# Output columns of a head on the quarter of its sums: the inverses of a softmax without a change of partition

## The chip, the cores and the metric

One core of a Trainium2 chip runs the whole kernel. The metric is the device time of one execution in microseconds (us); lower is better. Times are medians of several executions, and all runs compared here are in the fast state (granted TensorE clock 0.993 to 0.997 of full speed, averaged over a run).

## The reference, cut to what matters

Sixty-four batches of a 256 x 512 float32 matrix go through two layers. The first is multi-head attention over a graph with a residual and a layer norm, the second a graph convolution with the same. Only the attention is touched:

```python
q = (x @ Wq + bq).reshape(b, n, H, HD)                   # H = 8 heads, HD = 64
k = (x @ Wk + bk).reshape(b, n, H, HD)
v = (x @ Wv + bv).reshape(b, n, H, HD)
scores = jnp.einsum('bqhd,bkhd->bhqk', q, k) / jnp.sqrt(jnp.float32(HD))
scores = scores + (1.0 - adj)[None, None, :, :] * -1000000000.0
attn = jax.nn.softmax(scores, axis=-1)
out = jnp.einsum('bhqk,bkhd->bqhd', attn, v).reshape(b, n, d)
return out @ Wo + bo
# ... then x = layernorm(x + that), and a second layer of the same build
```

## The kernel before

It works on pairs of batches, 32 of them. A pair has four units, each one batch and one group of four heads. TensorE multiplies the values of a unit with the exponentials in four column groups of 32, side by side, each into its own quarter of the 128 partitions; it also sums the exponentials of each head into one quarter. In the kernel before, two neighbouring quarters belong to the two halves of one head, so that the sums of a head do not always stand where its outputs stand. Five small copies on ScalarE carry the inverse sums (1 over a sum of exponentials, by which softmax divides) to the quarters that need them:

```python
    def values(p, u):
        ...
        for a in range(2):
            for kc in range(NC):
                for s in range(2):
                    for r in range(2):
                        q, h = s * HD + r * 32, (2 * a + s) * HD + r * 32
                        nc.tensor.matmul(at[q:q + 32, 0, a, :], V[p, g][:, kc, b, h:h + 32], e[kc][:, s, a, :],
                                         start=kc == 0, stop=kc == NC - 1)
        for s in range(2):
            for a in range(2):
                q = s * HD + a * 32
                nc.tensor.matmul(at[q:q + 32, 1, 0, :], ones[:, 0:32], sm[:, s, a, :], start=True, stop=True)
        later(1, divided, p, u, at)

    def divided(p, u, at):
        ...
        nc.vector.transpose(z, at[:, 1, 0, :])                       # 256 elements per partition
        z1 = z.rearrange("p (j k) -> p j k", k=32)[:, :, 0]
        nc.vector.reciprocal(rz1, z1)
        nc.scalar.activation(rz, rz1[:, None, :].to_broadcast([P, 2, 8]), AF.Copy)
        for s in range(2):
            for a in range(2):
                here, there = (slice(s * HD + r * 32, s * HD + r * 32 + 32) for r in (a, 1 - a))
                nc.scalar.activation(rz[there, a], rz1[here], AF.Copy)
        nc.vector.transpose(rs, rz...)                               # 512 elements per partition
        nc.vector.tensor_tensor(O[p, g]..., at[:, 0]..., rs..., op=OP.mult)
        ...
```

ScalarE also reads the products of q out of PSUM, the memory into which TensorE writes; such a reading is called an eviction below. The kernel forms q from seven products of blocks and of sums of blocks. The third of them adds into the PSUM bank of the first, so it has to wait until the first was read:

```python
    SEVEN = [("a11", 0, 0, True), ("a12", 1, 1, True), ("s2", 4, 0, False), ...]   # name, block of w, bank, begins
    ...
        def first(to, pm, g):                                        # in q_or_k
            for a in range(2):
                nc.scalar.activation(to[:, a], pm[:, a], AF.Identity, bias=b[:, 2 * g + a:2 * g + a + 1])
```

The order of instructions on each engine is fixed when the kernel is built, by a scheduler that works with its own idea of when each operation is ready. At the start, VectorE forms four sums of blocks for each weight matrix, in the same queue as its additions to q, k and v.

Of the kernel before, what the change touches and what calls it, by code (L numbers as in the profile page):

```python
# [20 lines left out]
F32 = mybir.dt.float32  # L21
AF = mybir.ActivationFunctionType
OP = mybir.AluOpType
AX = mybir.AxisListType

P = 128
# [7 lines left out]
def tile_adj_resnorm(tc, x, adj, wq, bq, wk, bk, wv, bv, wo, bo, w1, b1, out):  # L34
    good = fast(tc, x, adj, wq, bq, wk, bk, wv, bv, wo, bo, w1, b1, out)
    with tc.If(good < P):
        general(tc, x, adj, wq, bq, wk, bk, wv, bv, wo, bo, w1, b1, out)


def fast(tc, x, adj, wq, bq, wk, bk, wv, bv, wo, bo, w1, b1, out):  # L40

    nc = tc.nc
    B, N, D = x.shape
    HD = D // H
    DC = D // P
    NC = N // P
    T2 = 2 * N
    NP = B // 2
    HF = D // 2
# [10 lines left out]
    cpool = pool("consts", 1)  # L60
    xpool = pool("xp", 4)
    rpool = pool("rp", 2)
    one = pool("one", 1)
    qk = pool("qk", 3)
    four = pool("four", 4)
    small = pool("small", 2)
# [3 lines left out]
    XC, R, XT, Q, K, V, E, SM, O, Y, ST = ({} for _ in range(11))  # L70
# [14 lines left out]
    ident = cpool.tile([P, P], F32, name="ident")  # L85
    make_identity(nc, ident)

    def weights(w, name):

        t = cpool.tile([P, 7, 2, HF], F32, name=name)  # L90
        b12 = one.tile([P, 2, HF], F32, name="b12")
        quarter = lambda k, n: w[k * HF:(k + 1) * HF, n * HF:(n + 1) * HF].rearrange("(c p) e -> p c e", p=P)
        nc.sync.dma_start(b12, quarter(0, 1))
        for i, (k, n) in enumerate(((0, 0), (1, 0), (1, 1))):
            nc.sync.dma_start(t[:, i], quarter(k, n))
        return t, b12

    def weight_sums(t, b12):
        b11, b21, b22, t1, t2, t3, t4 = (t[:, i] for i in range(7))
        nc.vector.tensor_tensor(t1, b12, b11, op=OP.subtract)  # L100
        nc.vector.tensor_tensor(t2, b22, t1, op=OP.subtract)
        nc.vector.tensor_tensor(t3, b22, b12, op=OP.subtract)
        nc.vector.tensor_tensor(t4, b21, t2, op=OP.subtract)

    def by_partition(b, name):
        t = cpool.tile([P, DC], F32, name=name)
        nc.scalar.dma_start(t, b.rearrange("(c p) -> p c", p=P))
        return t
# [3 lines left out]
        nc.scalar.dma_start(t, b.partition_broadcast(P))  # L112
        return t

    bq_s, bk_s, bv_s = by_partition(bq, "bq"), by_partition(bk, "bk"), by_partition(bv, "bv")
    W = {}
    for name, w in (("v", wv), ("q", wq), ("k", wk)):
        W[name], b12 = weights(w, "w" + name)
        weight_sums(W[name], b12)
# [3 lines left out]
    load_r(0)  # L123
    load_r(1)

    ones = cpool.tile([P, HD], F32, name="ones")
    nc.gpsimd.memset(ones, 1.0)
    power = cpool.tile([P, 4], F32, name="power")
    nc.gpsimd.memset(power, -0.5)
# [4 lines left out]
            nc.tensor.transpose(pt[:, mc, c * P:(c + 1) * P], adj_s[:, c, mc * P:(mc + 1) * P], ident)  # L134
    nc.vector.tensor_copy(adjT, pt)

    acc = cpool.tile([P, 16], F32, name="acc")
    square = one.tile([P, NC, N], F32, name="z")
    nc.vector.tensor_tensor(square, adj_s, adj_s, op=OP.mult)
    nc.vector.tensor_tensor(square, square, adj_s, op=OP.not_equal)  # L140
# [4 lines left out]
    def weights_of_outputs():  # L145
        W["1"], b12 = weights(w1, "w1")
        weight_sums(W["1"], b12)
        W["o"], b12 = weights(wo, "wo")
        weight_sums(W["o"], b12)

        wide = one.tile([P, DC, P], F32, name="z")
        nc.vector.tensor_copy(wide, bv_s[:, :, None].to_broadcast([P, DC, P]))
        pm = ps_mm.tile([P, 2, HF], F32, name="mm")
        for n, blocks in enumerate(((W["o"][:, 0], W["o"][:, 1]), (b12, W["o"][:, 2]))):
            for d in range(DC):
                nc.tensor.matmul(pm[:, n, :], wide[:, d, :], blocks[d // 2][:, d % 2, :], start=d == 0,
                                 stop=d == DC - 1)
        nc.vector.tensor_tensor(bo_s, bo_s, pm.rearrange("p n e -> p (n e)"), op=OP.add)
# [5 lines left out]
    def later(n, f, *args):  # L164
        due.append([n, f, args])

    def tick():
        for d in due:
            d[0] -= 1
        ready = [d for d in due if d[0] <= 0]  # L170
        due[:] = [d for d in due if d[0] > 0]
        for _, f, args in ready:
            f(*args)  # L173
# [7 lines left out]
    def row_sums(lo, hi, name):  # L181


        flat = lambda t: t.rearrange("p k b i -> p k (b i)")
        a11, a21, a12, a22 = flat(lo[:, 0]), flat(lo[:, 1]), flat(hi[:, 0]), flat(hi[:, 1])
        sums = one.tile([P, 3, 2, HF], F32, name=name)
        s1, s2, s4 = (sums[:, i] for i in range(3))
        for i, args in enumerate(((s1, a21, a22, OP.add), (s2, s1, a11, OP.subtract), (a21, a11, a21, OP.subtract),
                                  (s4, a12, s2, OP.subtract))):
            later(i + 1, nc.vector.tensor_tensor, *args)  # L190
        return dict(a11=a11, a12=a12, a22=a22, s1=s1, s2=s2, s3=a21, s4=s4)
# [71 lines left out]



    UNITS = [(g, b) for g in range(2) for b in range(2)]

    def scores(p, u):
        g, b = UNITS[u]
        for kc in range(NC):  # L270

            sc = ps_at.tile([P, 2, 2, N], F32, name="at")
            for a in range(2):
                for s in range(2):
                    r = slice(s * HD, (s + 1) * HD)
                    nc.tensor.matmul(sc[:, s, a, :], K[p, g][r, kc, a, b, :], Q[p, g][r, :, a, b, :],  # L276
                                     start=True, stop=True)
            e = E[p, u, kc] = one.tile([P, 2, 2, N], F32, name=f"e{kc}")
            nc.scalar.activation(e, sc, AF.Exp, scale=qscale)  # L279
            later(1 + kc, masked, p, u, kc)  # L280
# [11 lines left out]
    def values(p, u):  # L292
        g, b = UNITS[u]
        if (p, g) not in O:
            O[p, g] = four.tile([P, NC, 2, 2, P], F32, name="o")
        while (p, u) not in SM:
            tick()
        e = [E.pop((p, u, kc)) for kc in range(NC)]
        sm = SM.pop((p, u))
        at = ps_at.tile([P, 2, 2, N], F32, name="at")  # L300
        for a in range(2):
            for kc in range(NC):
                for s in range(2):
                    for r in range(2):
                        q, h = s * HD + r * 32, (2 * a + s) * HD + r * 32
                        nc.tensor.matmul(at[q:q + 32, 0, a, :], V[p, g][:, kc, b, h:h + 32], e[kc][:, s, a, :],  # L306
                                         start=kc == 0, stop=kc == NC - 1)
        for s in range(2):
            for a in range(2):
                q = s * HD + a * 32  # L310
                nc.tensor.matmul(at[q:q + 32, 1, 0, :], ones[:, 0:32], sm[:, s, a, :], start=True, stop=True)  # L311
        later(1, divided, p, u, at)

    def divided(p, u, at):


        g, b = UNITS[u]
        z = one.tile([P, N], F32, name="z")
        nc.vector.transpose(z, at[:, 1, 0, :])
        z1 = z.rearrange("p (j k) -> p j k", k=32)[:, :, 0]  # L320
        rz1 = small.tile([P, 8], F32, name="rz1")
        nc.vector.reciprocal(rz1, z1)  # L322
        rz = small.tile([P, 2, 8], F32, name="rz")
        nc.scalar.activation(rz, rz1[:, None, :].to_broadcast([P, 2, 8]), AF.Copy)  # L324
        for s in range(2):
            for a in range(2):
                here, there = (slice(s * HD + r * 32, s * HD + r * 32 + 32) for r in (a, 1 - a))
                nc.scalar.activation(rz[there, a], rz1[here], AF.Copy)  # L328
        rs = one.tile([P, T2], F32, name="rs")
        nc.vector.transpose(rs, rz.rearrange("p a j -> p (a j)")[:, :, None].to_broadcast([P, 16, 32]))  # L330
        nc.vector.tensor_tensor(O[p, g][:, :, :, b, :].rearrange("p c a i -> p a c i"), at[:, 0].rearrange("p a (c i) -> p a c i", c=NC),
                                rs.rearrange("p (a c i) -> p a c i", a=2, c=NC), op=OP.mult)
        seen = small.tile([P, 8], F32, name="seen")
        nc.gpsimd.tensor_tensor(seen, rz1, z1, op=OP.add)
        nc.gpsimd.tensor_tensor(acc[:, 0:8], acc[:, 0:8], seen, op=OP.add)
        if u == 3:
            O[p] = row_sums(O.pop((p, 0)), O.pop((p, 1)), "ys")

# [85 lines left out]
    for w in range(-1, NP + 1):  # L424
        steps = between(w)
        slots = [(f, w, u) for u in range(4) for f in (scores, values)] if 0 <= w < NP else []
        whole, done, n = sum(s[0] for s in steps), 0.0, len(slots)
        while steps or slots:
            if slots and done >= whole * (n - len(slots)) / n - 1e-6:
                f, p, u = slots.pop(0)  # L430
                f(p, u)
            elif steps:
                t, f, p, i = steps.pop(0)
# [3 lines left out]
            else:  # L437
                f, p, u = slots.pop(0)
# [4 lines left out]
    while due:  # L443
        tick()

    good = one.tile([P, 16], F32, name="good")
    nc.vector.tensor_scalar(good, acc, RANGE, None, op0=OP.is_le)
    least = one.tile([P, 1], F32, name="least")
    nc.vector.tensor_reduce(least, good, AX.X, OP.min)
    count = ps_mm.tile([P, 1], F32, name="mm")  # L450
    nc.tensor.matmul(count[0:HD], ones, least, start=True, stop=True)
    n_good = one.tile([1, 1], mybir.dt.int32, name="n_good")
    nc.vector.tensor_copy(n_good, count[0:1])
    got = nc.values_load(n_good[0:1, 0:1], min_val=0, max_val=P,
# [178 lines left out]
```

## Time and profile before

| | before |
|---|---|
| time, median of 3 runs | 2889.97 us (2887.91 to 2893.08) |
| TensorE busy | 98% |
| VectorE busy | 65% |
| ScalarE busy | 28% |

The prediction below shows and reads the lines. What to take from them first is that TensorE is the bound, so that a change to VectorE or ScalarE counts only where TensorE waits for them.

To read the lines: PE is TensorE, DVE VectorE, ACT ScalarE, and SPq is a queue that issues loads. A line of a timeline begins with its start and its duration in us; a bracket gives the idle time before it and what ended that. The trace has two records for each float32 matmul: a unit has 16 matmuls of values in the code and 32 in the trace (x4096 for 128 units).

### The profile page before, as it was taken

Reading aid. Unit: us, or ns where it says so; the run is one execution under the profiler, and the core shown is the slowest. Engines: PE = TensorE matmul, PEld = TensorE weight load, DVE = VectorE, ACT = ScalarE, POOL = GpSimd, SP = SyncE. Lnnn points to the kernel's source line nnn. Section 1 sums busy time; section 2 is a strip of 40 time slices with the busy share of each in tenths; the row PEclk is TensorE's granted clock in tenths of the full one; section 3 lists DMA queues with packets and bytes.
Section 4 is the critical chain, followed back from the end, with each engine's and each line's share of the span. In section 5 each row is a group of like instructions: output and inputs, shape, how many; then the busy total and the mean of one; then the engine's idle time right before and its main releaser. Section 6 shows DMA issues by size and latency. Waiting matters only on the chain.

```text
span 2886.5 us, 41721 instructions
## 1 busy us (share of the span) xinstructions
PE 2831.1 (98%) x17686; PEld 2278.7 (79%) x17686; DVE 1874.4 (65%) x3007; ACT 812.2 (28%) x1793; POOL 168.5 (6%) x328
## 2 busy tenths in 40 slices
PE   8999999999999999999999999999999999999997
PEld 6787788877778878787887788778877887877775
DVE  5566666666666667666666666676665666666666
ACT  2322232222223323222232223222222222222220
POOL 0000000000000000000000000000000000000000
PEclk9999999999999999999999999999999999999998
DMA  4000111101111001111011110111100111101000
GB/s 157 16 30 15 45 45 45 45 1 45 44 45 44 15 30 45 45 45 45 1 45 44 45 44 8 37 45 44 45 31 15 45 44 45 44 1 44 30 30 30
DMA packets 60510, 109.43 MB, mean 38 GB/s; under 512 B 5536, under 2 KB 10912, under 8 KB 60320
## 3 DMA queue, kind: packets, MB, share of 16 engines
q1 hardware_dynamic: 58176, 105.92, 11.0%
q8 instruction: 141, 2.31, 0.3%
q10 hardware_dynamic: 2144, 0.79, 0.1%
q14 instruction: 49, 0.40, 0.0%
HBM read 73.14 MB, written 33.55 MB: 37 GB/s over the span
## 4 chain that ended last, share of the span: by engine, by line
PE 79%; DVE 11%; DMA 5%; POOL 2%; ACT 2%; issue 1%; SPq 0%; POOLq 0%; ACTq 0%; DVEq 0%
PE mm L205 56%; PE mm L399 8%; PE at L276 8%; PE at L306 5%; DVE r L367 3%; DMA r<-in_x_dram 3%; DVE st L352 2%; POOL rstd L360 2%; DMA out_dram<-r 2%; DVE r L378 1%; PE at L311 1%; PE mm L218 1%; DVE r L343 1%; ACT rz L328 1%; DVE ys L173 1%; ACT qT L244 1%
## 5 line engine op out<-in xcount | busy, mean ns | idle before, releaser
L284 DVE TENSOR_TENSOR e<-e,adjT 128x1024 f32<-128x1024 f32 x256 | 304.5, 1220 | 116.7 <-ACT e L279 116.6
L279 ACT ACTIVATE e<-at 128x1024 f32<-128x1024 f32 x256 | 248.3, 1021 | 222.7 <-PE at L276 216.1
L276 PE MATMUL at<-qT,kT 64*128 64x256 f32 x2048 | 256.0, 389 | 0.0
L231 DVE TENSOR_TENSOR r<-r,mm 128x512 f32<-128x512 f32 x192 | 130.7, 681 | 184.3 <-PE mm L205 182.1
L399 PE MATMUL mm<-adjT,r 128*128 128x256 f32 x1024 | 239.8, 388 | 8.4 <-issue 4.5
L306 PE MATMUL at<-e,v 128*32 128x256 f32 x4096 | 247.7, 382 | 0.0
L205 PE MATMUL mm<-wv,xT 128*128 128x256 f32 x1024 | 244.4, 382 | 0.0
L205 PE MATMUL mm<-wo,o 128*128 128x256 f32 x1024 | 243.1, 380 | 0.3 <-DVE o L173 0.3
L205 PE MATMUL mm<-w,o 128*128 128x256 f32 x1024 | 242.0, 379 | 0.0
L205 PE MATMUL mm<-xT,wk 128*128 128x256 f32 x1024 | 241.7, 379 | 0.0
L205 PE MATMUL mm<-xT,wq 128*128 128x256 f32 x1024 | 240.2, 382 | 0.0
L324 ACT ACTIVATE rz<-rz 128x16 f32<-128x16 f32 x128 | 27.6, 216 | 748.7 <-DVE rz L322 747.7
L244 ACT ACTIVATE kT<-mm,bk 128x256 f32<-128x256 f32 x256 | 107.2, 470 | 453.1 <-PE mm L205 453.1
L276 PEld LDWEIGHTS at<-qT,kT 64*128 64x128 f32 x2048 | 187.2, 186 | 59.9 <-issue 42.9
L399 PEld LDWEIGHTS mm<-adjT,r 128*128 128x128 f32 x1024 | 195.5, 193 | 45.7 <-issue 15.1
L205 PEld LDWEIGHTS mm<-xT,wq 128*128 128x128 f32 x1024 | 191.9, 190 | 37.9 <-issue 13.1
L205 PEld LDWEIGHTS mm<-wv,xT 128*128 128x128 f32 x1024 | 196.0, 192 | 27.7 <-issue 0.5
L205 PEld LDWEIGHTS mm<-w,o 128*128 128x128 f32 x1024 | 194.3, 190 | 27.5 <-issue 1.2
L205 PEld LDWEIGHTS mm<-xT,wk 128*128 128x128 f32 x1024 | 194.5, 190 | 26.8 <-issue 0.4
L205 PEld LDWEIGHTS mm<-wo,o 128*128 128x128 f32 x1024 | 191.7, 190 | 27.0 <-issue 1.1
L378 DVE TENSOR_TENSOR r<-r,mm 128x512 f32<-128x512 f32 x256 | 174.4, 681 | 48.3 <-PE mm L205 44.0
L306 PEld LDWEIGHTS at<-e,v 128*32 128x32 f32 x4096 | 119.9, 109 | 108.6 <-issue 41.8
(92 smaller groups left out, 3873.1 us busy)
## 6 DMA issues: line engine op xcount, KB each, us to landing
xc<-in_x_dram SPq DMA_DIRECT2D x128, 256.0 KB, 3.7
r<-in_x_dram SPq DMA_DIRECT2D x32, 1024.0 KB, 6.3
out_dram<-r SPq DMA_DIRECT2D x64, 512.0 KB, 3.6
wv<-in_L_gnn_Wv_dram SPq DMA_DIRECT2D x3, 256.0 KB, 5.1
wq<-in_L_gnn_Wq_dram SPq DMA_DIRECT2D x3, 256.0 KB, 5.6
wk<-in_L_gnn_Wk_dram SPq DMA_DIRECT2D x3, 256.0 KB, 5.3
w<-in_L_gnn_weight_dram SPq DMA_DIRECT2D x3, 256.0 KB, 5.2
wo<-in_L_gnn_Wo_dram SPq DMA_DIRECT2D x3, 256.0 KB, 6.2
```

Of the source, the lines that this page charges most:

```text
L205: nc.tensor.matmul(pm[:, j, :], left[:, k, j * P:(j + 1) * P], right[:, k, :], start=begins and j == 0 and k == 0, stop=k == 1, skip_group ...
L231: nc.vector.tensor_tensor(to, to, pm, op=OP.add)
L244: nc.scalar.activation(to[:, a], pm[:, a], AF.Identity, bias=b[:, 2 * g + a:2 * g + a + 1])
L276: nc.tensor.matmul(sc[:, s, a, :], K[p, g][r, kc, a, b, :], Q[p, g][r, :, a, b, :], start=True, stop=True)
L279: nc.scalar.activation(e, sc, AF.Exp, scale=qscale)
L284: nc.vector.tensor_tensor(e, e, adjT[:, kc:kc + 1, :].to_broadcast([P, 4, N]), op=OP.mult)
L306: nc.tensor.matmul(at[q:q + 32, 0, a, :], V[p, g][:, kc, b, h:h + 32], e[kc][:, s, a, :], start=kc == 0, stop=kc == NC - 1)
L352: nc.vector.bn_stats(st, R[p][:, b, c, :])
L360: nc.gpsimd.tensor_tensor(rstd, ve, power, op=OP.pow)
L367: nc.vector.tensor_scalar(R[p][:, b, c, :], R[p][:, b, c, :], mv[:, i, 0:1], rstd[:, i:i + 1], op0=OP.subtract, op1=OP.mult)
L378: assembled(i, pm, out, lambda to, pm, half: nc.vector.tensor_tensor(to, to, pm, op=OP.add))
L399: nc.tensor.matmul(pm[:, j, :], R[p][:, b, mc, d * P:(d + 1) * P], adjT[:, mc, :], start=mc == 0, stop=mc == NC - 1)
```

## The change

The intent is to let a head's 64 output columns lie in two slices of 32 on the one quarter where its sums stand. Then no inverse has to change partition, the five copies go, and the second transpose is half as long. The price is that the rows of wo, and bv, have to be loaded in the same order.

```diff
-    def weights(w, name):
+    def weights(w, name, by_head=False):
 ...
+            if by_head:
+                for a in range(2):
+                    nc.sync.dma_start(to[:, a], quarter.rearrange("(h a i) e -> a h i e", h=4, a=2)[a])
+            else:
+                nc.sync.dma_start(to, quarter.rearrange("(c p) e -> p c e", p=P))
 ...
+    for d in range(DC):
+        nc.scalar.dma_start(bv_s[:, d:d + 1], bv.rearrange("(g h a i u) -> g a h i u", h=4, a=2, i=32, u=1)[d // 2, d % 2])
 ...
-        W["o"], b12 = weights(wo, "wo")
+        W["o"], b12 = weights(wo, "wo", True)
 ...
+                for h in range(4):
+                    col = h * HD + a * 32
+                    nc.tensor.matmul(at[h * 32:(h + 1) * 32, 0, a, :], V[p, g][:, kc, b, col:col + 32],
+                                     e[kc][:, h % 2, h // 2, :], start=kc == 0, stop=kc == NC - 1)
+        for h in range(4):
+            nc.tensor.matmul(at[h * 32:(h + 1) * 32, 1, 0, :], ones, sm[:, h % 2, h // 2, :], start=True, stop=True)
 ...
-        nc.scalar.activation(rz, rz1[:, None, :].to_broadcast([P, 2, 8]), AF.Copy)
-        for s in range(2):
-            for a in range(2):
-                here, there = (slice(s * HD + r * 32, s * HD + r * 32 + 32) for r in (a, 1 - a))
-                nc.scalar.activation(rz[there, a], rz1[here], AF.Copy)
-        rs = one.tile([P, T2], F32, name="rs")
-        nc.vector.transpose(rs, rz.rearrange("p a j -> p (a j)")[:, :, None].to_broadcast([P, 16, 32]))
+        rs = one.tile([P, N], F32, name="rs")
+        nc.vector.transpose(rs, rz[:, :, None].to_broadcast([P, N // 32, 32]))
 ...                                            (the product then repeats rs over a)
```

More of the change, by code (lines that the diff above doesn't have):

```diff
@@ L86, in fast @@
     make_identity(nc, ident)
-    def weights(w, name):
+    def weights(w, name, by_head=False):
         t = cpool.tile([P, 7, 2, HF], F32, name=name)
         b12 = one.tile([P, 2, HF], F32, name="b12")
-        quarter = lambda k, n: w[k * HF:(k + 1) * HF, n * HF:(n + 1) * HF].rearrange("(c p) e -> p c e", p=P)
-        nc.sync.dma_start(b12, quarter(0, 1))
-        for i, (k, n) in enumerate(((0, 0), (1, 0), (1, 1))):
-            nc.sync.dma_start(t[:, i], quarter(k, n))
+        for to, k, n in ((b12, 0, 1), (t[:, 0], 0, 0), (t[:, 1], 1, 0), (t[:, 2], 1, 1)):
+            quarter = w[k * HF:(k + 1) * HF, n * HF:(n + 1) * HF]
+            if by_head:
[3 more added lines that the diff above has]
+                nc.sync.dma_start(to, quarter.rearrange("(c p) e -> p c e", p=P))
         return t, b12
@@ L113, in on_all @@
         return t
-    bq_s, bk_s, bv_s = by_partition(bq, "bq"), by_partition(bk, "bk"), by_partition(bv, "bv")
+    bq_s, bk_s = by_partition(bq, "bq"), by_partition(bk, "bk")
+    bv_s = cpool.tile([P, DC], F32, name="bv")
+    for d in range(DC):
+        nc.scalar.dma_start(bv_s[:, d:d + 1], bv.rearrange("(g h a i u) -> g a h i u", h=4, a=2, i=32, u=1)[d // 2, d % 2])
     W = {}
@@ L124, in fast @@
     load_r(1)
-    ones = cpool.tile([P, HD], F32, name="ones")
+    ones = cpool.tile([P, 32], F32, name="ones")
     nc.gpsimd.memset(ones, 1.0)
@@ L135, in fast @@
     nc.vector.tensor_copy(adjT, pt)
-    acc = cpool.tile([P, 16], F32, name="acc")
+    acc = cpool.tile([P, N // 32], F32, name="acc")
     square = one.tile([P, NC, N], F32, name="z")
@@ L302, in values @@
             for kc in range(NC):
-                for s in range(2):
-                    for r in range(2):
-                        q, h = s * HD + r * 32, (2 * a + s) * HD + r * 32
-                        nc.tensor.matmul(at[q:q + 32, 0, a, :], V[p, g][:, kc, b, h:h + 32], e[kc][:, s, a, :],
-                                         start=kc == 0, stop=kc == NC - 1)
-        for s in range(2):
-            for a in range(2):
-                q = s * HD + a * 32
-                nc.tensor.matmul(at[q:q + 32, 1, 0, :], ones[:, 0:32], sm[:, s, a, :], start=True, stop=True)
+                for h in range(4):
[4 more added lines that the diff above has]
+            nc.tensor.matmul(at[h * 32:(h + 1) * 32, 1, 0, :], ones, sm[:, h % 2, h // 2, :], start=True, stop=True)
         later(1, divided, p, u, at)
@@ L320, in divided @@
         z1 = z.rearrange("p (j k) -> p j k", k=32)[:, :, 0]
-        rz1 = small.tile([P, 8], F32, name="rz1")
-        nc.vector.reciprocal(rz1, z1)
-        rz = small.tile([P, 2, 8], F32, name="rz")
-        nc.scalar.activation(rz, rz1[:, None, :].to_broadcast([P, 2, 8]), AF.Copy)
-        for s in range(2):
-            for a in range(2):
-                here, there = (slice(s * HD + r * 32, s * HD + r * 32 + 32) for r in (a, 1 - a))
-                nc.scalar.activation(rz[there, a], rz1[here], AF.Copy)
-        rs = one.tile([P, T2], F32, name="rs")
-        nc.vector.transpose(rs, rz.rearrange("p a j -> p (a j)")[:, :, None].to_broadcast([P, 16, 32]))
-        nc.vector.tensor_tensor(O[p, g][:, :, :, b, :].rearrange("p c a i -> p a c i"), at[:, 0].rearrange("p a (c i) -> p a c i", c=NC),
-                                rs.rearrange("p (a c i) -> p a c i", a=2, c=NC), op=OP.mult)
-        seen = small.tile([P, 8], F32, name="seen")
-        nc.gpsimd.tensor_tensor(seen, rz1, z1, op=OP.add)
-        nc.gpsimd.tensor_tensor(acc[:, 0:8], acc[:, 0:8], seen, op=OP.add)
+        rz = small.tile([P, N // 32], F32, name="rz")
+        nc.vector.reciprocal(rz, z1)
+        rs = one.tile([P, N], F32, name="rs")
+        nc.vector.transpose(rs, rz[:, :, None].to_broadcast([P, N // 32, 32]))
+        nc.vector.tensor_tensor(O[p, g][:, :, :, b, :].rearrange("p c a i -> p a c i"),
+                                at[:, 0].rearrange("p a (c i) -> p a c i", c=NC),
+                                rs.rearrange("p (c i) -> p c i", c=NC)[:, None].to_broadcast([P, 2, NC, P]), op=OP.mult)
+        seen = small.tile([P, N // 32], F32, name="seen")
+        nc.gpsimd.tensor_tensor(seen, rz, z1, op=OP.add)
+        nc.gpsimd.tensor_tensor(acc, acc, seen, op=OP.add)
         if u == 3:
@@ L444, in fast @@
         tick()
-    good = one.tile([P, 16], F32, name="good")
+    good = one.tile([P, N // 32], F32, name="good")
     nc.vector.tensor_scalar(good, acc, RANGE, None, op0=OP.is_le)
@@ L450, in fast @@
     count = ps_mm.tile([P, 1], F32, name="mm")
-    nc.tensor.matmul(count[0:HD], ones, least, start=True, stop=True)
+    nc.tensor.matmul(count[0:32], ones, least, start=True, stop=True)
     n_good = one.tile([1, 1], mybir.dt.int32, name="n_good")
```

## The prediction

> **What bounds the kernel now.** I read first the page's busy line, to see which engine could set the time; then the waits of TensorE, to see what it is still held up by; then one of those waits in the timeline; last the groups of instructions that the change touches.
>
> ```profile
> PE 2831.1 (98%) x17686; PEld 2278.7 (79%) x17686; DVE 1874.4 (65%) x3007; ACT 812.2 (28%) x1793; POOL 168.5 (6%) x328
> ```
>
> TensorE (PE) is busy 98% of 2886.5 us; VectorE (DVE) has a third of the span free, ScalarE (ACT) two thirds. Since the ends of matmuls in a trace are modelled, I checked the 98% against starts. Eight consecutive 128x256 matmul records of a block product (L205) start 1.727 us before the next eight, 0.216 us each, over hundreds of such groups. Taking 0.216 us as the price of a full-width record, a half of it for the scores' records (two run side by side) and a quarter for the values' and the sums' (four side by side), all TensorE work comes to some 2735 us. About 150 us lie above that: some 0.1 us at most changes of tile shape, the start and the tail, and stalls. Only those 150 us can be won by a change that leaves the matmuls alone.
>
> The waits of TensorE, then the two waits that the change is aimed at (us in total, times, longest):
>
> ```profile
> PE mm L205 <- ACT qT L244: 14.5, 30, 0.5
> PE mm L134 <- DMA rs<-in_adj_dram: 7.1, 1, 7.1
> PE mm L205 <- DVE r L378: 5.0, 10, 1.8
> ...
> DVE rs L330 <- ACT rz L328: 115.2, 99, 1.2
> ```
>
> One stall comes back: 30 times, once in nearly every pair of batches, TensorE waits 0.48 us for ScalarE to read a q block out of PSUM (L244). The 115 us that VectorE waits for the inverses (rs after rz) look larger, but VectorE isn't the bound. What ties the two together is the timeline around one of the 30:
>
> ```profile
> 1567.00 0.61 PE L311 MATMUL at<-sm,ones 128*32 128x256 f32 x8
> ...
> 1567.54 3.72 PE L205 MATMUL mm<-xT,wq 128*128 128x256 f32 x16
> ...
> 1569.72 0.21 ACT L324 ACTIVATE rz<-rz 128x16 f32<-128x16 f32 x1 [3.77 <-DVE rz L322]
> ...
> 1569.97 0.86 ACT L328 ACTIVATE rz<-rz 32x8 f32<-32x8 f32 x4
> ...
> 1570.85 0.84 ACT L244 ACTIVATE qT<-mm,bq 128x256 f32<-128x256 f32 x2
> ...
> 1571.74 1.99 PE L205 MATMUL mm<-xs,wq 128*128 128x256 f32 x8 [0.48 <-ACT qT L244]
> ...
> 1573.57 3.62 PE L399 MATMUL mm<-adjT,r 128*128 128x256 f32 x16
> ```
>
> ScalarE stands idle until VectorE's reciprocal is there, does the five small copies of the inverses, and only then the two evictions of q. The first eight q matmuls were over at about 1569.4, so these evictions could have begun then. The third q product adds into the same PSUM bank and has to wait for them. The copies that the change removes are thus the cause of the only repeated stall of TensorE.
>
> **What the Trainium skill says.** "TensorE: Matmul & The Clock Gate", section "Back-to-back issue gap", puts an isolated 512-column matmul at about 216 ns; here one record of a 256-column f32 matmul takes the same 216 ns, so TensorE runs at the rate of its array and nothing in its instructions is left to win. "TensorEngine Tiling (Array Packing)", section "Key Properties", says that changing the tiling mode drains TensorE; this trace agrees with some 0.1 us lost at most such changes, and the change leaves their number as it is. "ScalarE: Activation LUTs", section "What ACT_TABLE_LOAD costs", gives an activation with immediate scale 186 ns plus 0.833 ns per element: 193 ns for 8 elements, 206 measured here, so nearly all of a copy's time is fixed cost. "Vector Engine (DVE) Microarchitecture Reference", section 3.8, has the 32x32 transpose at one element per cycle and lane; the trace's two sizes, 710 and 447 ns, differ by 263 ns for 256 elements, about one per ns.
>
> **The change part by part.** The groups that it touches (busy us, mean ns of one | idle before):
>
> ```profile
> L306 PE MATMUL at<-e,v 128*32 128x256 f32 x4096 | 247.7, 382 | 0.0
> L311 PE MATMUL at<-sm,ones 128*32 128x256 f32 x1024 | 78.7, 379 | 0.2 <-DVE sm L290 0.2
> L324 ACT ACTIVATE rz<-rz 128x16 f32<-128x16 f32 x128 | 27.6, 216 | 748.7 <-DVE rz L322 747.7 <-DVE ve L358 1.0
> L328 ACT ACTIVATE rz<-rz 32x8 f32<-32x8 f32 x512 | 105.6, 206 | 8.5
> L330 DVE STREAM_TRANSPOSE rs<-rz 128x512 f32<-128x512 f32 x128 | 90.9, 710 | 115.2 <-ACT rz L328 115.2
> L319 DVE STREAM_TRANSPOSE z<-at 128x256 f32<-128x256 f32 x128 | 57.2, 447 | 113.1 <-PE at L311 113.1
> ```
>
> 1. The values' matmuls: as many as before, 2 (a) x 2 (key chunks) x 4 (column groups), each 32 columns wide into its own quarter. What is new is that four neighbours stream four different heads, where before two streamed the same. The order of the quarters is kept, as is that of the sums. TensorE: 0.
> 2. The copies on ScalarE go: 27.6 + 105.6 = 133 us, so ScalarE falls from 812 to about 679 us, and 640 instructions go. By themselves worth nothing.
> 3. The second transpose is halved: 128 x (710 - 447) ns = 34 us, if 256 elements from SBUF take what they take from PSUM. VectorE falls from 1874 to about 1840 us; its 115 us of waits for L328 vanish. From the first transpose to the end of the division takes 3.3 us when nothing comes between (70.50 to 73.78 in the first unit), then about 0.45 + 0.20 + 0.45 + 0.69 and small gaps, 1.85 us. The multiplication stays at 512 elements, 688 ns; that one operand is now repeated costs nothing that I can read from the trace.
> 4. The stall. From 1567.54 to 1573.57 are 6.03 us for 24 records. Without the stall: 24 x 0.216 = 5.18, plus 0.10 for the change of tile shape ahead of them, 5.28. Each of the 30 stalls thus costs 0.75 us, more than the 0.48 that the waits show[...]. With the copies gone the evictions begin at about 1569.6 and end at 1570.45; the weights of the third product are due at about 1570.8. The stall vanishes whole: 30 x 0.75 = 22.5 us.
> 5. The 10 short waits for r (L378), 5.0 us, come from VectorE waiting for the residual's DMA and stay.
> 6. Start: the one load of bv becomes four, ahead of adj on the same issuing queue at 0.53 us each, so adj is 1.6 us later. But TensorE's first longer work is held until 15.46 us by a copy (L135) that VectorE does only after the first weights (in at 12.9). Estimate +0.5 us. wo comes in eight loads instead of four, long before its use at 54.9 us: 0.
> 7. Tail: after the last values VectorE works without a break up to the row sums that TensorE waits for (1.86 us at 2837.04). A shorter division brings them forward by some 0.8 us of idle time and 0.26 us of transpose: -1.
>
> Sum: -22.5 + 0.5 - 1 = -23, from 2890 to **2867 us** (-0.8%).
>
> **The rivals.** *The order of instructions changes against us.* The order on each engine is settled when the kernel is built, and depends on when operations are thought to be ready. At present VectorE does the reciprocal between the two additions of bo, just ahead of the eviction of r (L378) that TensorE waits for. If the transpose and the multiplication, 1.1 us and now ready at once, slip in there too, the 10 short waits become 30 of up to 1 us: +20 to +30 us, the gain is gone, about 2890 us. Against it: these additions and the eviction come earlier in the program, and the division was taken only where they weren't ready. *Another engine or buffer takes the wait over.* Should the q product wait as long for something else, only the 1 us of the tail remains, 2889 us. Against it: ScalarE has nothing else to do between 1565.95 and the evictions, and the PSUM buffers of the values already come free more than 1 us before the next scores want them. *Four different streams are slower on TensorE.* Were the values' 128 x 1.75 us a tenth slower, +22 us. Against it: the sums' matmuls already stream four different blocks, eight records in 0.43 us, the same rate. *More than that:* a shorter division could also do away with the waits for r, 2861 us; I see no path from one to the other.
>
> **Range and chances.** The central term is nearly fixed by counting, and runs of one kernel differ by about 5 us. The first two rivals reach up to the old time or a little above, so the range is wider on that side: **2860 to 2885 us**. For 2% (2832 us) there would have to be 58 us of gain, and the repeated stall has 22: faster 0.02. Slower by 2% would need a new stall of over 2 us in each pair: 0.02. Within 2%: 0.96.
>
> **What would show it.** Right: no wait of L205 for ACT qT; 24 q records in about 5.3 us after the sums; VectorE's 256-element transposes at about 0.45 us; busy ScalarE about 679 us and VectorE 1840; busy TensorE almost as before in microseconds; a period of a pair of 87.6 us rather than 88.3. Wrong: many more or longer waits of L205 for r (L378), a values group of clearly over 1.75 us, or waits of the scores for the division. I would be mistaken altogether if the time fell by over 40 us, which would mean that the busy time of TensorE hid stalls that I didn't count.

## The result, and the profile after

The changed kernel takes 2875.43 us (median of 4 runs, 2874.71 to 2880.03), the kernel before 2888.94 us beside it. Ratios here are the mean time of one kernel's fast runs over that of the other's fast runs of the same rounds, so not quite the ratio of the medians. This one is 0.9955, with a 95% interval of 0.9937 to 0.9972: faster by about 13 us, clear of noise but inside 2%. The time lies in the predicted range; the centre, 2867 us, was 8 us too low.

The busy line of the page of the changed kernel:

```profile
PE 2824.3 (98%) x17686; PEld 2280.1 (79%) x17686; DVE 1854.6 (65%) x3007; ACT 680.5 (24%) x1153; POOL 168.5 (6%) x328
```

ScalarE fell from 812 to 680.5 us, as worked out (679). The groups that the change touches, from the view by line and form; line numbers have moved (L306 is now L313, L311 is L316, L330 is L328, L319 is L323):

```profile
L313 PE MATMUL at<-e,v 128*32 128x256 f32 x4096 | 247.6, 382 | 0.0
L316 PE MATMUL at<-sm,ones 128*32 128x256 f32 x1024 | 78.7, 379 | 0.2 <-DVE sm L298 0.2
L323 DVE STREAM_TRANSPOSE z<-at 128x256 f32<-128x256 f32 x128 | 57.3, 448 | 113.0 <-PE at L316 113.0
L328 DVE STREAM_TRANSPOSE rs<-rz 128x256 f32<-128x256 f32 x128 | 56.8, 444 | 3.4
```

The values cost what they did (247.7 and 247.6 us), so four column groups that stream four different heads are not slower. The second transpose takes 444 ns, where 447 were expected, and its 115 us of waiting are gone. Now the repeated stall, in the same place of the repeated part as the prediction's timeline:

```profile
1567.15 0.61 PE L316 MATMUL at<-sm,ones 128*32 128x256 f32 x8
1567.69 3.72 PE L212 MATMUL mm<-xT,wq 128*128 128x256 f32 x16
...
1569.72 0.84 ACT L251 ACTIVATE qT<-mm,bq 128x256 f32<-128x256 f32 x2 [3.62 <-PE mm L212]
...
1571.25 1.89 PE L212 MATMUL mm<-xs,wq 128*128 128x256 f32 x8
1572.97 3.62 PE L398 MATMUL mm<-adjT,r 128*128 128x256 f32 x16
```

The evictions of q begin as soon as the first product is there, and end at 1570.56. The third product follows the second without a gap. From 1567.69 to 1572.97 are 5.28 us, where before it was 6.03: the 0.75 us that the prediction had counted.

So where are the other 10 us? I compared the starts of the sums' matmuls, 128 groups in each trace, one for each unit, in the same order in both kernels. The first and the last before:

```profile
67.89 0.61 PE L311 MATMUL at<-sm,ones 128*32 128x256 f32 x8
...
2827.46 0.61 PE L311 MATMUL at<-sm,ones 128*32 128x256 f32 x8
```

and after:

```profile
78.21 0.61 PE L316 MATMUL at<-sm,ones 128*32 128x256 f32 x8
...
2815.65 0.61 PE L316 MATMUL at<-sm,ones 128*32 128x256 f32 x8
```

The first group starts at 67.89 us before and 78.21 us after: **10.3 us late, before the repeated part has begun**. The last one starts at 2827.46 before and 2815.65 after, 11.8 us early. In between 22.1 us were won, where 22.5 were predicted. From there to the end of the span another 1.3 us are won. The account is +10.3 - 22.1 - 1.3 = -13.1 us, the difference of the two spans (2886.5 and 2873.4).

The waits in the changed trace name the place (us in total, times, longest):

```profile
DVE wo L104 <- DMA b<-in_L_gnn_Wo_dram: 7.8, 1, 7.8
...
PE mm L141 <- DMA rs<-in_adj_dram: 10.4, 1, 10.4
...
PE mm L212 <- DVE qT L238: 5.7, 1, 5.7
...
PE mm L212 <- DVE r L377: 3.3, 8, 1.8
```

The 30 waits for qT are not there. The short waits for r have stayed (8 for 10). New are a wait of TensorE of 5.7 us, once, and a longer one for adj, 10.4 us in place of 7.1. The timeline of the start shows the order of events, first in the kernel before:

```profile
34.49 0.37 SPq L93 DMA_DIRECT2D b<-in_L_gnn_Wo_dram  x1
...
37.35 0.69 DVE L100 TENSOR_TENSOR wo<-b,wo 128x512 f32<-128x512 f32 x1 [1.35 <-DMA b<-in_L_gnn_Wo_dram]
...
39.89 0.69 DVE L231 TENSOR_TENSOR qT<-qT,mm 128x512 f32<-128x512 f32 x1
...
41.34 1.89 PE L205 MATMUL mm<-xs,wq 128*128 128x256 f32 x8
```

and in the changed one:

```profile
30.66 5.71 SPq L97 DMA_DIRECT2D wo<-in_L_gnn_Wo_dram  x6
...
37.17 2.24 SPq L97 DMA_DIRECT2D b<-in_L_gnn_Wo_dram  x2
...
46.13 0.69 DVE L104 TENSOR_TENSOR wo<-b,wo 128x512 f32<-128x512 f32 x1 [7.79 <-DMA b<-in_L_gnn_Wo_dram]
...
48.67 1.28 DVE L238 TENSOR_TENSOR qT<-qT,mm 128x512 f32<-128x512 f32 x2
49.40 3.78 PE L212 MATMUL mm<-xs,wq 128*128 128x256 f32 x8 [5.69 <-DVE qT L238]
```

The product that uses wo comes much later, but VectorE forms the sums of its blocks here, ahead of an addition to q, and it takes its work in order. A late wo therefore holds q, and q holds TensorE. The eight matmuls after the stall take 3.78 us in place of 1.89; the granted clock is 0.62 in the windows from 46 to 55 us.

The DMA engines in windows of the changed kernel (after the busy times, the last three columns are the clock, the busy share of the 16 DMA engines, and GB/s):

```profile
30.00:34.00 4.00, 4.00 (x20) 3.54 (x19) 1.38 (x2) 0.60 (x1) 0.00 (x0) 1.00 1.07 356
...
38.00:42.00 4.00, 4.00 (x20) 3.54 (x19) 0.34 (x1) 1.68 (x4) 0.00 (x0) 1.00 0.27 94
42.00:46.00 4.00, 1.71 (x8) 1.15 (x7) 0.00 (x0) 0.00 (x0) 0.00 (x0) 1.00 0.22 76
```

At 30 to 34 us other loads move 356 GB/s on all engines. Once wo alone is left, the share is about a quarter, as if 4 engines worked all the time (0.27 x 16 = 4.3), at 94 GB/s. At this rate the 1.05 MB of wo take 11 us. The issuing doesn't hold them up: the last of these loads was issued by 39.4 us, and VectorE got its block at 46.1.

The Trainium skill has a rule that fits this. "DMA: Bandwidth & Descriptors", section "Why a DMA increments its semaphore by 16 and not by 1", says that a copy is spread over the largest number of engines, up to 16, that divides the slowest dimension of both its sides. The source here is walked as 4 heads x 32 rows x 256 elements, so the number is 4. I had not looked this page up before predicting.

### The profile page after: what moved, and what is told of

Read it like the earlier page. It is cut to its first block, busy times and chain, and to the rows that moved or that the text cites. A ratio compares the mean times of both kernels' runs of the same rounds, so it can differ in the third digit from the quotient of the medians.

```text
span 2873.4 us, 41408 instructions
## 1 busy us (share of the span) xinstructions
PE 2824.3 (98%) x17686; PEld 2280.1 (79%) x17686; DVE 1854.6 (65%) x3007; ACT 680.5 (24%) x1153; POOL 168.5 (6%) x328
## 4 chain that ended last, share of the span: by engine, by line
PE 88%; DMA 5%; DVE 5%; POOL 1%; issue 0%; SPq 0%; ACTq 0%; POOLq 0%; DVEq 0%
PE mm L212 62%; PE mm L398 8%; PE at L284 8%; PE at L313 7%; DMA r<-in_x_dram 2%; PE at L316 2%; DMA out_dram<-r 1%; PE mm L225 1%; DVE r L342 1%; DVE r L366 1%; POOL rstd L359 1%; DVE ys L180 1%; DVE st L351 1%; DVE r L377 1%; DMA wv<-in_L_gnn_Wv_dram 0%
## 5 line engine op out<-in xcount | busy, mean ns | idle before, releaser
L313 PE MATMUL at<-e,v 128*32 128x256 f32 x4096 | 247.6, 382 | 0.0
L263 ACT ACTIVATE v<-mm 128x512 f32<-128x512 f32 x128 | 76.4, 597 | 673.4 <-PE mm L212 673.4
L212 PEld LDWEIGHTS mm<-xT,wq 128*128 128x128 f32 x1024 | 191.9, 190 | 37.9 <-issue 13.1
L251 ACT ACTIVATE qT<-mm,bq 128x256 f32<-128x256 f32 x256 | 107.3, 470 | 456.4 <-PE mm L212 456.4
```

The costliest lines, as they stand in the source:

```text
L212: nc.tensor.matmul(pm[:, j, :], left[:, k, j * P:(j + 1) * P], right[:, k, :], start=begins and j == 0 and k == 0, stop=k == 1, skip_group ...
L263: assembled(i, pm, out, lambda to, pm, g: nc.scalar.activation(to, pm, AF.Copy))
L313: nc.tensor.matmul(at[h * 32:(h + 1) * 32, 0, a, :], V[p, g][:, kc, b, col:col + 32], e[kc][:, h % 2, h // 2, :], start=kc == 0, stop=kc = ...
```

## The experiments

There are two theories to test. **Q**: the repeated gain comes from nothing but ScalarE's copies no longer standing ahead of the evictions of q. **L**: the loss at the start comes from the loads of wo and bv. In every run "before" is the kernel before, beside it on the same chip.

| run | what it is | median us | ratio to before (95%) |
|---|---|---|---|
| changed kernel | | 2875.43 | 0.9955 (0.9937 to 0.9972) |
| e1_even_odd | other split of the columns, one load each | 2865.89 | 0.9916 (0.9902 to 0.9929) |
| e2_wo_plain | wo in the old order (wrong) | 2868.03 | 0.9924 (0.9910 to 0.9937) |
| e3_bv_plain | bv in one load | 2871.99 | 0.9938 (0.9925 to 0.9952) |
| e4_before_copies_dve | before, copies on VectorE | 2865.45 | 0.9920 (0.9904 to 0.9936) |
| e5_copies_unread | changed, copies back, unread | 2898.55 | 1.0030 (1.0017 to 1.0044) |
| e6_full_transpose | changed, second transpose at 512 | 2874.97 | 0.9953 (0.9940 to 0.9966) |
| e7_wo_by_head_32 | changed, wo in 16 loads, 32 first | 2863.47 | 0.9917 (0.9902 to 0.9932) |
| e8_wo_pairs | changed, wo in 16 loads, 2 first | 2877.08 | 0.9957 (0.9943 to 0.9971) |

Before ran at 2889.03 to 2889.82 us beside them.

**The copies back, read by nobody.** Edit to the changed kernel:

```diff
         nc.vector.reciprocal(rz, z1)
+        spare = small.tile([P, 2, 8], F32, name="spare")
+        nc.scalar.activation(spare, rz[:, None, :].to_broadcast([P, 2, 8]), AF.Copy)
+        for s in range(2):
+            for a in range(2):
+                here, there = (slice(s * HD + r * 32, s * HD + r * 32 + 32) for r in (a, 1 - a))
+                nc.scalar.activation(spare[there, a], rz[here], AF.Copy)
```

> The changed kernel with the five small copies of the inverses back on ScalarE, at the same place, into a tile that nothing reads; the division doesn't wait for them. Theory Q (the repeated stall came from the copies standing ahead of the evictions of q on ScalarE): the 30 waits of TensorE for qT are back, +30 x 0.75 = 22 us, 2898 us. Rival D (the gain comes from the shorter division on VectorE): unchanged, 2875 us.

It took 2898.55 us, 23 us more than the changed kernel, slower than before even, since it pays the start as well. In the waits of TensorE the old line is back:

```profile
PE mm L212 <- ACT qT L251: 14.2, 30, 0.5
```

The division doesn't wait for these copies, and it is still as short as in the changed kernel. The theory of the shorter division falls.

**The kernel before with the copies on VectorE.** Edit: the two `nc.scalar.activation(..., AF.Copy)` of `divided` become `nc.vector.tensor_copy`, nothing else.

> The kernel before, with nothing changed but the engine of the five small copies of the inverses: VectorE does them, in the same place between reciprocal and second transpose. Loads, matmuls and sizes are those of before. Theory Q (the repeated stall is the copies standing ahead of the evictions of q on ScalarE): no waits of TensorE for qT, 2889 - 22 = 2867 us, though VectorE has 128 x 5 instructions and over 60 us more to do. Rival D (the gain is that of a shorter division on VectorE): not faster than 2889 us.

It took 2865.45 us, and its busy line reads

```profile
PE 2821.0 (99%) x17686; PEld 2278.9 (80%) x17686; DVE 1985.5 (69%) x3647; ACT 680.8 (24%) x1153; POOL 169.0 (6%) x328
```

VectorE has 111 us more to do than before, and the kernel is 24 us faster. None of its TensorE waits is for qT. The whole gain of the repeated part comes with moving the copies to another engine, and none of the loss. Theory Q holds from both sides.

The traces say the same of the repeated part alone. From the first to the last group of sums takes 2759.6 us before and 2758.4 with the copies back, but 2735.8 with the copies on VectorE, and 2735.0 to 2738.6 in the changed kernel and the six other runs.

**The second transpose at its old size.** Edit to the changed kernel: `rs` is a tile of 512 again, and the transpose reads the inverses twice.

> The changed kernel with the second transpose at its old size, 512 elements: VectorE gets its 34 us back, everything else stays. Theory Q: VectorE isn't the bound and nothing in the repeated part waits for the division, so the time stays at 2875 us, give or take 2. Rival D (part of the gain is VectorE's): slower by up to 10 us.

It took 2874.97 us, no different from 2875.43, with VectorE busy 1885.8 us instead of 1854.6. Thirty microseconds of VectorE are worth nothing here.

**wo in its old order.** Edit to the changed kernel: `weights(wo, "wo", True)` becomes `weights(wo, "wo")`. The result is wrong (relative error 0.48).

> The changed kernel with wo loaded in its natural order of rows, in four loads of 256 KB as before; the result is wrong on purpose. Theory L: the late half of the loss at the start is the stall of 5.7 us behind VectorE's wait for wo, with a colder clock after it, 7.6 us in all; time 2875.4 - 7.6 = 2868 us, and no stall near 45 us. Rival A (order of instructions, not the loads): stall stays, 2875 us.

It took 2868.03 us, 7.4 less. One wait of 1.1 us for qT is left near 44 us in place of 5.7.

**bv in one load.** Edit to the changed kernel: `bv_s = by_partition(bv, "bv")`, as before.

> The changed kernel with bv in one load as before (bv is zero in this data, so the result stays right). Theory L: adj comes 3 us earlier and so does the first work of TensorE after it (15.5 and not 18.15 us); the loads of the weights follow the same chain, so the wait for wo comes earlier by as much: 2875.4 - 2.7 = 2872.7 us. Rival: the 2.7 us are hidden behind the later wait for wo, 2875 us.

It took 2871.99 us, 3.4 less, though its interval overlaps that of the changed kernel, so the time alone doesn't show it. The trace does: the wait for adj is 7.1 us again, and TensorE takes up its work at 15.80 us after the wait for adjT, where it does at 18.15 in the changed kernel and at 17.35 to 18.28 in the five other runs that load bv in four. By the medians the two loads cost 7.4 + 3.4 us; by the first sums in the traces (71.3 and 75.9 us in place of 78.2) 6.9 + 2.3, for 10.3 in all. These parts are rough: the runs with the copies back and with the full transpose, whose loads are those of the changed kernel, start their sums at 76.4 and 78.1. That both loads have a part is shown by the even-odd version below, with both mended, which starts its sums at 67.7 us, as the kernel before does, while the run with 32 rows first, which still loads bv in four, starts them at 69.4. Theory L holds; how the 10.3 us divide is known to some 2 us only.

**Wo by head in 16 loads, 32 rows first.** The same rows on the same partitions:

```diff
-                for a in range(2):
-                    nc.sync.dma_start(to[:, a], quarter.rearrange("(h a i) e -> a h i e", h=4, a=2)[a])
+                for h in range(4):
+                    nc.sync.dma_start(to[h * 32:(h + 1) * 32], quarter[h * HD:(h + 1) * HD].rearrange("(a i) e -> i a e", a=2))
```

> The changed kernel with the same rows of wo on the same partitions, but loaded head by head: 16 loads of 64 KB with 32 partitions as their first dimension, where the changed kernel has 8 of 128 KB with the 4 heads as their first. Theory F (a load whose first dimension is 4 runs on only 4 of the 16 DMA engines: the trace shows a share of 0.22 to 0.27 and 76 to 94 GB/s between 38 and 46 us): the loads move at several times that rate, are over soon after their issue, the first block of wo lands at about 41.5 us and not 46, the stall shrinks to some 1 us, about 2869 us. Rival N (what costs is the number of loads, each with a fixed price): 16 loads are worse than 8, 2880 us or more.

It took 2863.47 us (2861.83 to 2871.72), better than expected: its trace has no stall for q at the start at all. It has twice as many loads as the changed kernel, so the number of loads isn't what costs. But its loads are also half as large and issued in another order, which the next run holds fixed in part.

**Wo in 16 loads of the same size, 2 heads first.**

```diff
                 for a in range(2):
-                    nc.sync.dma_start(to[:, a], quarter.rearrange("(h a i) e -> a h i e", h=4, a=2)[a])
+                    for hh in range(2):
+                        nc.sync.dma_start(to[hh * 64:(hh + 1) * 64, a], quarter.rearrange("(g h a i) e -> g a h i e", g=2, a=2, i=32)[hh, a])
```

> The changed kernel with wo in 16 loads of 64 KB, as many and as large as in the run with 32 partitions first, the same rows on the same partitions, but each load takes two heads, so its first dimension is 2 (2 heads x 32 rows x 1 KB). Theory F (a load is spread over as many DMA engines as its first dimension has steps): only 2 engines work, a DMA share of about 0.13 and some 47 GB/s while wo alone is loaded, half the rate of the changed kernel (94); 1.05 MB take 22 us and not 11, the first block of wo comes up to 10 us later than in the changed kernel, and the time is about 2885 us. Rival S (what made the run with 32 first fast is the smaller size of a load or the other order of issue): as fast as that one, 2864 us.

The same windows of the run with 2 first:

```profile
38.00:42.00 4.00, 4.00 (x21) 3.51 (x20) 0.00 (x0) 1.50 (x4) 0.00 (x0) 1.00 0.14 47
42.00:46.00 4.00, 0.97 (x5) 0.51 (x3) 0.00 (x0) 0.00 (x0) 0.00 (x0) 1.00 0.13 47
```

and of the run with 32 first:

```profile
38.00:42.00 4.00, 4.00 (x21) 3.51 (x20) 1.23 (x3) 1.51 (x4) 0.00 (x0) 1.00 0.48 125
42.00:46.00 4.00, 4.00 (x20) 3.54 (x19) 2.63 (x5) 0.84 (x2) 0.00 (x0) 1.00 0.24 72
```

The share of two engines (0.14 x 16 = 2.2) and 47 GB/s, half of what the changed kernel moved. That is the forecast to the number, and bears out the theory, though the views show a share of 16 engines and not which of them work. A rival, that the issuing sets the pace (1.2 us for one load, median), falls in the same trace: the last load was issued by 48.7 us, and from 50 to 54 us the rate is still 47 GB/s. The time, 2877.08 us, is 8 us better than I expected: the first block of wo landed at 48.6 us, only 2.5 us later than in the changed kernel, since it was issued after 7 of the 16 loads and not after 6 of 8. VectorE's second wait, for another block at 55.6 us, held no one. The run with 32 first shows how long its loads take in the clear (2.0 us from issue to landing, median); its rates in these windows (125 and 72 GB/s) can't exceed that of the issuing, one load of 64 KB every 0.43 us or about 150 GB/s, so they don't show how many engines such a load could use.

**A version without the loss.** If a head's columns are split into even and odd ones instead of halves, then partition 32h + i needs rows 64h + 2i and 64h + 2i + 1 of wo: neighbours in memory. One load for each quarter of wo does, with the 128 partitions first, and one load for bv. The values' weights are then every second column of v:

```diff
-                    nc.tensor.matmul(at[h * 32:(h + 1) * 32, 0, a, :], V[p, g][:, kc, b, col:col + 32],
+                    nc.tensor.matmul(at[h * 32:(h + 1) * 32, 0, a, :], V[p, g][:, kc, b, h * HD:(h + 1) * HD].rearrange("p (i a) -> p a i", a=2)[:, a],
 ...
+                nc.sync.dma_start(to, quarter.rearrange("(p a) e -> p a e", a=2))
 ...
+    nc.scalar.dma_start(bv_s.rearrange("p (g a) -> p g a", a=2), bv.rearrange("(g p a) -> p g a", p=P, a=2))
```

> The changed kernel with another split of a head's columns: even and odd ones, not first and second half. A quarter of wo then lies in memory as two neighbouring rows to each partition, so that one load of 256 KB over 128 partitions does for it (4 loads for wo again, not 8), and one load does for bv. Theory L (the changed kernel loses about 10 us at the start to its loads and wins 22 us in the steady part): the start is as in the kernel before, scores begin at about 58.7 us and not 69.0, time 2875 - 10 = 2865 us. Rival A (the 10 us at the start are the price of something else, the new order of instructions): 2875 us. Rival B (weights taken from every second column of v load slower and TensorE pays): the group of 32 value matmuls takes over 1.75 us and part of the gain is gone; at 10% that is 128 x 0.175 = 22 us, 2887 us.

It took 2865.89 us, correct, and beats both kernels: 9.5 us less than the changed one. Scores begin at 58.55 us. Weights with a stride of two columns load in 111 ns on average, where 109 were measured before, and the values' matmuls take 247.8 us.

This version, the run with 32 rows first and the kernel before with its copies on VectorE have overlapping intervals; which of the three is best isn't settled.

## Why the prediction was right or wrong

Two figures of the prediction come out differently when they are redone; no term of its sum rests on them. With its prices, the records of the page add up to about 2710 us of TensorE work and not 2735 (10,000 full-width records, 2048 of scores, 5120 of values and sums, 512 transposes at a half), so that some 175 us lie above and not 150. And 2% are 58 us, 1.8 us in each of 32 pairs and not over 2.

1. *Values' matmuls: 0.* Right, 247.7 and 247.6 us.
2. *ScalarE loses 133 us, by itself worth nothing.* Right in size (132 us).
3. *The second transpose loses 34 us.* Right for the group (90.9 to 56.8 us), and worth nothing, as the run with the full transpose shows. VectorE's busy time fell by 20 us only, not 34. Busy time counts overlapping neighbours once: the durations by themselves add up to 2031.5 us before and 2001.2 after, 30 less, and the part that overlaps fell from 157 to 147 us.
4. *The stall vanishes whole, 30 x 0.75 = 22.5 us.* Right: 22.1 us between first and last sums. Its cause is shown by putting the copies back (+23 us) and by moving them (-24 us).
5. *The short waits for r stay.* Right, 8 waits and 3.3 us after 10 and 5.0.
6. *Start: +0.5 us, of which wo 0.* **This is the step that failed**: it measured +10.3. In it were two errors. The loads of wo were taken to be due at their matmul at 54.9 us, but the first that needs them is VectorE, which at 37.35 us forms the block sums and has only 2.5 us of work between them and an addition that TensorE needs soon after. And the loads were taken to run at the usual rate, when by the rule cited above their shape put them on 4 engines of 16. For bv the 1.6 us of issuing were seen, but adj was issued 3.2 us later (5.56 for 2.34) as one of the four issues took 1.1 us and there was a pause behind them; and the slack that I saw in the wait for the first weights was none, as those came later too (15.6 for 12.9).
7. *Tail: -1 us.* Right, -1.3, and the wait that it named is 0.89 us after 1.86. From the last sums to the end takes 59.0 us before and 58.9 to 59.1 in the three runs with the copies or the long transpose in place, 56.8 to 58.0 in the others.

Of the rivals, the first (an unlucky order of instructions) did not come about in the repeated part. The second (another wait) fell with point 4, the third (slower streams) with point 1, and the hope of more, that the waits for r go too, with point 5. The mechanism and its size were right; the sum was off by the start alone. That the range still held is luck in part: its upper side was left wide for the first two rivals, which didn't come about, and the 10 us of the start, which no rival named, fell into that room.

## What to carry to other kernels

When one engine is the bound, look for who holds it, not for who waits longest: 0.75 us, 30 times, behind five small copies on an otherwise idle engine was worth 22 us, and 115 us of VectorE's waiting were worth nothing. In an in-order queue a small operation that waits for another engine delays everything behind it, so moving it to an engine that already has its input can do as much as removing it. When a load's layout changes, ask how many DMA engines its first dimension can use, and which instruction in which queue is the first to need it.

## What the Trainium skill lacked or had wrong

- "DMA: Bandwidth & Descriptors", section "Why a DMA increments its semaphore by 16 and not by 1", had the rule right, and the runs agree: first dimension 4 gave a share of 0.22 to 0.27 and up to 94 GB/s, 2 gave 0.13 to 0.14 and 47 GB/s, about 23.5 GB/s for each engine by the rule. What the page doesn't say is that such a load can take longer to issue: up to 1.66 us in the changed kernel, where those of the weights in the kernel before took 0.37 to 0.56.
- "TensorEngine Tiling (Array Packing)", section "Key Properties", says that a change of tiling mode drains TensorE but not what that costs: about 0.1 us at most of the changes here.
- "TensorE: Matmul & The Clock Gate" doesn't say whether four column groups cost more when they stream four different operands. Here they don't: 247.6 us, and 247.7 when pairs of them stream the same.
